# Two attention layers on one core: where the loads for the next batch are issued in layer 1

## The chip, the cores and the metric

The kernel runs on one NeuronCore of a Trainium2 chip. The metric is the time on the device of one execution, in microseconds; lower is better. The kernel before takes 3918.9 us, the median of three runs from 3916.26 to 3920.2 us.

The engines are named as in the profile: PE (TensorE: matrix products), ACT (ScalarE), DVE (VectorE), POOL (GpSimd) and SP (SyncE, which only issues transfers). Sixteen DMA engines move data between DRAM and the on-chip memory (SBUF) and within it.

## The reference

Eight images x of 512 channels and 32 x 32 = 1024 positions go through two residual layers, all in float32. Layer 0 is an ordinary attention with eight heads and does not matter here. Layer 1 is an attention whose heads are mixed before the softmax and normalised after it:

```
q, k, v = einsum('oc,bct->bot', w_q | w_k | w_v, gn(x))      # 8 heads of 64 channels
attn = einsum('bhdq,bhdT->bhqT', q, k) * scale
attn = einsum('gh,bhqT->bgqT', w_head, attn)                 # each head becomes a mix of all eight
attn = softmax(attn, axis=-1)
attn = (attn - mean) / sqrt(var + EPS) * in_gamma + in_beta  # mean and var per image and head
out  = einsum('bhqT,bhdT->bhqd', attn, v).reshape(b, t, c) @ w_proj.T + b_proj
x = x + out
```

## The kernel before, in words

Layer 0 runs from 0 to about 1790 us, layer 1 from there to the end. Layer 1 loops over eight batches b = 0..7 (one image each), and inside a batch over steps p = 0..8 (`step`, called for p and for t = 0..3). A step handles 128 of the 1024 query positions. The steps are numbered from 0 here, as in the code: "step 3" is p = 3, the fourth step of the batch. Work of several query blocks overlaps: in step p the kernel makes the raw scores of block p, mixes and exponentiates block p - 1, and multiplies block p - 2 (and the beginning of p - 1) with the values v.

- `scores(p, i)`, i = 0..7 (L1674): q times k for one pair of heads and one half of the keys. The half is kh = i // 4. ACT copies each result from PSUM into the tile `raw` (L1686), which has one buffer for each half.
- `regroup(p, kh, s)` (L1692): two transfers of 256 KB each, issued by SP, from `raw` to the tile `re`, so that the eight heads of one position come to lie on neighbouring partitions. A step issues 16 of them: three pairs of half 0 at t = 1, one pair at t = 2, four pairs of half 1 at t = 3. Half 1 can be copied only when the last scores of the step are done, so its pairs are issued in fact at the very end of step p and in the first 5 us of step p + 1.
- `mix(p, s)`, s = 0..3 (L1711): PE multiplies `re` with the mixing matrix; ACT takes the exponential (L1724). `mix(p, 0)` is called in step p + 1 at t = 0, behind three scores and a piece of values; it needs the first pair of half 1.
- `flip` (L1739) and `moments` (L1753) on DVE, `values` (L1769) on PE, and `leave` (L1785) on ACT follow.
- At the odd steps 3, 5 and 7, `totals` (L1811 to L1817) makes the reciprocal sums of a pair of blocks, and POOL's queue writes them to DRAM (`zd`, four transfers of 2 KB). `broadcast` (L1829) is written in the program at steps 4, 6 and 8, t = 0 and t = 2, and reads them back as two transfers of 256 KB (`rzb`), also from POOL's queue. POOL does nothing else in between, so it issues them as soon as the four small writes have landed. `divide` (L1856) on POOL uses them.

The order of the work on every engine is the order of the program text, written out by hand in `step`. A small agenda (`ag`) holds extra work with the slot at which it is to run: `y` of the next batch is normalised at step 6, one of its four parts in each t; the k projection of the next batch starts in step 8.

The change is about the loads for the next batch. Each is a closure in the list `pieces`, and `piece(n)` (L1696 to L1700) runs the next n of them. For batches 0 to 6 there are six pieces of 512 KB each: four parts of `y` of the next batch (`y_piece`, L1349) and two of the four parts of its k weights (`left_piece`, L1318, f = 0 and f = 4). The first k piece also takes the tile `left`, whose last reader was the q projection before the batch. The other two parts of the k weights come at step 8 from the agenda. For batch 7 there are four pieces of 256 KB each, the output weights (`p_piece`, L1343). All pieces are issued by SP, at t = 0 of a step, so they stand in SP's queue behind the half-1 regroups of the step before and ahead of the half-0 regroups of their own step.

The setup of the pieces and the loop that calls `step`:

```
a.pieces += [lambda c=c: y_piece(b + 1, c) for c in range(NCC)]
a.pieces += [lambda f=f: left_piece(("k", b + 1), f, 2) for f in (0, 4)]
...
a.pieces += [lambda c=c: p_piece(c) for c in range(NCC)]      # last batch
...
for p in range(NT + 1):
    for t in range(4):
        a.step(p, t, ag)
```

Of the kernel before, what the change touches and what calls it, by code (L numbers as in the profile page):

```python
# [467 lines left out]
def tile_two_attention_layers(  # L468
# [810 lines left out]
    with ExitStack() as l1:  # L1279
# [173 lines left out]
        def k_leave():  # L1453
            for fn in due:
                fn()
            due.clear()
# [203 lines left out]
        class Attention1:  # L1660
# [242 lines left out]
            def step(self, p, t, ag):  # L1903

                new, old, older = p < NT, p >= 1, p >= 2
                if t == 0:
                    if new:
                        for i in range(3):
                            self.scores(p, i)
                            if i == 1:  # L1910
                                ag.run(4 * p - 0.75)
                    if older:
                        self.values(p - 2, 0, 2, 3)
                        self.leave(p - 2, 0)
                        if p % 2:
                            self.sums(p // 2 - 1)
                    ag.run(4 * p - 0.5)
                    k_leave()
                    if old:
                        self.mix(p - 1, 0)  # L1920
                    ag.run(4 * p - 0.25)
                    if p % 2 == 0 and p >= 4:
                        self.broadcast(0)
                elif t == 1:
                    if older:
                        self.values(p - 2, 1, 0)
                        self.flip(p - 1, 0)
                        if p % 2:
                            self.totals(p // 2 - 1)
                        self.moments(p - 1, 0)  # L1930
                    if new:
                        self.scores(p, 3)
                    ag.run(4 * p + 0.5)
                    k_leave()
                    if old:
                        self.mix(p - 1, 1)
                elif t == 2:
                    if p % 2 == 0 and p >= 4:
                        self.broadcast(1)
                    if older:  # L1940
                        self.values(p - 2, 1, 1)
                    if new:
                        self.scores(p, 4)
                        self.scores(p, 5)
                    ag.run(4 * p + 1.5)
                    k_leave()
                    if old and not new:
                        self.mix(p - 1, 2)
                    if older:
                        self.values(p - 2, 1, 2, 3)  # L1950
                        self.leave(p - 2, 1)
                    if old and new:
                        self.mix(p - 1, 2)
                else:
                    if new:
                        self.scores(p, 6)
                        if old:
                            self.values(p - 1, 0, 0)
                        self.scores(p, 7)
                        if old:  # L1960
                            self.mix(p - 1, 3)
                            self.values(p - 1, 0, 1)
                    else:
                        ag.run(4 * p + 2.5)
                        k_leave()
                        self.mix(p - 1, 3)
                        self.values(p - 1, 0, 0, 1)
                if p == 1 or old and t:
                    self.flip(p - 1, t)
                    self.moments(p - 1, t)  # L1970
                if new:
                    first = 3 + (p == 0)
                    for kh, s in (
                        [], [(0, i) for i in range(first)], [(0, i) for i in range(first, 4)],
                        [(1, i) for i in range(4)],
                    )[t]:
                        self.regroup(p, kh, s)
                if t == 3 and p % 2 == 0 and p >= 4:
                    self.divide(p // 2 - 2, nc.gpsimd)
                if older and t == 0:  # L1980
                    self.piece()
                ag.run(4 * p + t)

        def set_flag(pf):
# [172 lines left out]
```

## Time and profile before

| | |
|---|---|
| median of three runs | 3918.9 us (3916.26 to 3920.2) |
| the profiled execution: time, and span of its instructions | 3922.93 us, 3921.2 us |
| PE busy | 3862.0 us, 98% of the span |
| DVE, ACT, POOL busy | 2736.8, 1968.0, 207.3 us |
| transfers issued by SP (queue q1) | 500.08 MB, 45.0% of 16 engines' span |
| transfers issued by POOL (queue q0) | 12.81 MB, 1.6% |
| regroups | 1024 transfers of 256 KB |
| waits of PE in layer 1, from 1820 us on, for a regroup to land | 12.5 us in 14 waits |

How to read it. The span runs from the first to the last instruction of the profiled execution. Busy time says how long an engine had something to do; PE's 98% leaves some 59 us of idle time in the whole kernel. "a <- b" after a group names what ended the wait before it. The share of the DMA engines is the mean over sixteen engines of the time in which they had a packet in hand. Step boundaries are taken at the first score product (L1674) of each step. SP's instructions are all issues and waits, so the landing of its transfers is read from the updates of their semaphores in the trace.

### The profile page before, as it was taken

The numbers are of one execution on the slowest core, as the hardware profiler recorded it, in microseconds if no ns is written. First come the engines' busy times: TensorE is split into PE (matmuls) and PEld (weight loads), VectorE is DVE, ScalarE is ACT, GpSimd is POOL, SyncE is SP. The second block draws the span as 40 slices with busy tenths as digits, with TensorE's granted clock in tenths as the row PEclk, the third lists the DMA queues.
The fourth block names the chain that finished last, engine by engine and source line by source line (L and its number), as shares of the span: only waits on it lengthen the run. The fifth ranks groups of instructions, "written<-read, shape, count | busy, mean of one in ns | idle before, by whom it ended". The sixth has DMA issues, their size and how long they took to land. (4 is left out here: it accounts for less than half of the span.)

```text
span 3921.2 us, 95349 instructions
## 1 busy us (share of the span) xinstructions
PE 3862.0 (98%) x41868; PEld 1818.7 (46%) x41868; DVE 2736.8 (70%) x3729; ACT 1968.0 (50%) x2400; POOL 207.3 (5%) x210
## 2 busy tenths in 40 slices
PE   8999999999999999999999999999999999999999
PEld 4353534344353535344554544535545545445455
DVE  4747576665757474766867858858858768678498
ACT  1726354453627172534725717627438257166175
POOL 0000000000000000000110200201101102002000
PEclk9999999999999999999999999999999999999999
DMA  3313131212121121215947929749659569387396
GB/s 121 120 54 117 49 116 36 71 48 85 55 75 67 49 87 49 90 49 149 235 144 178 243 83 231 200 124 235 187 129 233 158 162 234 107 216 207 120 220 161
DMA packets 249592, 519.07 MB, mean 132 GB/s; under 512 B 51024, under 2 KB 58192, under 8 KB 242512
## 3 DMA queue, kind: packets, MB, share of 16 engines
q1 hardware_dynamic: 241984, 500.08, 45.0%
q0 software_dynamic: 7184, 12.81, 1.6%
q8 instruction: 330, 5.41, 0.6%
q14 instruction: 94, 0.77, 0.1%
HBM read 197.16 MB, written 46.92 MB: 62 GB/s over the span
## 5 line engine op out<-in xcount | busy, mean ns | idle before, releaser
L1739 DVE STREAM_TRANSPOSE et<-e 128x2048 f32<-128x2048 f32 x256 | 590.0, 2305 | 197.4 <-ACT e L1724 196.5
L1769 PEld LDWEIGHTS a<-et,v 128*64 128x64 f32 x16384 | 506.6, 138 | 287.7 <-issue 272.7
L1753 DVE BATCH_NORM_STATS2 bn<-e 128x6 f32<-128x512 f32 x1024 | 635.7, 683 | 0.0
L1093 ACT ACTIVATE e<-s 128x1024 f32<-128x1024 f32 x512 | 497.1, 1026 | 232.7 <-PE s L1088 229.5
L1686 ACT COPY raw<-s 128x1024 f32<-128x1024 f32 x480 | 470.1, 1018 | 234.9 <-PE s L1674 208.7
L1724 ACT ACTIVATE e<-m 128x1024 f32<-128x1024 f32 x512 | 496.3, 1021 | 164.9 <-issue 62.2
L1769 PE MATMUL a<-et,v 128*64 128x64 f32 x16384 | 554.8, 224 | 3.3 <-issue 3.2
L1103 DVE TENSOR_TENSOR zacc<-zacc,e 128x1024 f32<-128x1024 f32 x384 | 468.8, 1221 | 123.7 <-ACT e L1093 99.4
L1674 PE MATMUL s<-k,q 64*64 64x512 f32 x4096 | 514.4, 606 | 2.7 <-DVE v L1046 1.4
L1088 PE MATMUL s<-q,k 64*64 64x512 f32 x4096 | 490.4, 594 | 2.3 <-ACT e L1093 2.3
L1116 PE MATMUL a<-e,v 64*64 64x512 f32 x4096 | 484.1, 589 | 0.0
L1711 PE MATMUL m<-re,wmix 32*32 32x512 f32 x8192 | 304.7, 599 | 17.7 <-DMA re<-raw 12.5
L1116 PEld LDWEIGHTS a<-e,v 64*64 64x64 f32 x4096 | 156.7, 133 | 282.8 <-issue 282.2
L1088 PEld LDWEIGHTS s<-q,k 64*64 64x64 f32 x4096 | 146.4, 133 | 284.3 <-issue 217.8
L1817 POOL DMA_DIRECT2D zd<-rz x96 | 52.5, 552 | 3378.4 <-DMA re<-raw 1862.5
L1674 PEld LDWEIGHTS s<-k,q 64*64 64x64 f32 x4096 | 127.3, 132 | 216.3 <-issue 97.2
L1785 ACT COPY q<-a 64x256 f32<-64x256 f32 x256 | 94.1, 367 | 136.8 <-PE a L1769 135.1
L1711 PEld LDWEIGHTS m<-re,wmix 32*32 32x32 f32 x8192 | 67.9, 103 | 156.6 <-ACT raw L1686 70.6
L1482 PE MATMUL pv_t<-wv,y 128*128 128x512 f32 x256 | 120.6, 608 | 0.0
L906 PE MATMUL pv_p<-left_v,tmp 128*128 128x256 f32 x512 | 114.7, 380 | 2.5 <-DVE tmp L935 2.5
L906 PE MATMUL pk_p<-tmp,left_k 128*128 128x512 f32 x256 | 112.5, 592 | 0.0
L906 PE MATMUL pq_p<-tmp,left_q 128*128 128x512 f32 x256 | 112.5, 592 | 0.0
(325 smaller groups left out, 3838.8 us busy)
## 6 DMA issues: line engine op xcount, KB each, us to landing
re<-raw SPq DMA_DIRECT2D x1024, 256.0 KB
left_q<-left_q SPq DMA_DIRECT2D x17, 1792.0 KB
left_p<-left_p SPq DMA_DIRECT2D x17, 1792.0 KB
left_k<-left_k SPq DMA_DIRECT2D x10, 1792.0 KB
x<-in_x_dram SPq DMA_DIRECT2D x32, 512.0 KB
rzb<-zd SPq DMA_DIRECT2D x128, 128.0 KB
x<-x SPq DMA_DIRECT2D x64, 256.0 KB
y<-x SPq DMA_DIRECT2D x32, 512.0 KB
```

The source lines that it names most:

```text
L906: nc.tensor.matmul(out, st, mv, start=start, stop=(k == 1), skip_group_check=True)
L1088: nc.tensor.matmul(ps[c * D : c * D + D, m], k[r, hp, k0 : k0 + D], q[r, hp, ts(f, FB)], start=True, stop=True,)
L1093: nc.scalar.activation(e[i], ps, AF.Exp, scale=S0 * S0)
L1103: nc.vector.tensor_add(zacc[g], zacc[g], e[i])
L1116: nc.tensor.matmul(acc[g][a][m * D : m * D + D], v[rows, kc, ts(2 * hp + m, D)], e[i][rows, m], start=(kc == 0), stop=(kc == NG - 1),)
L1674: nc.tensor.matmul(ps[c * D : c * D + D, m], qo_t[b][r, p, hp, ts(c, D)], k_t[b][r, hp, ts(kh, FB)], start=True, stop=True,)
L1686: nc.scalar.copy(dst, ps)
L1711: nc.tensor.matmul(ps[a // 2][c * 32 : c * 32 + 32, a % 2].rearrange("p (r h k) -> p h r k", r=2, h=2), wmix[rows].rearrange("p g i -> p ( ...
L1724: nc.scalar.activation(e[:, :, 2 * h : 2 * h + 2].rearrange("p r a k -> p a r k"), ps[h].rearrange("p a (r k) -> p a r k", r=2), AF.Exp,)
L1739: nc.vector.transpose(self.et[p, u].rearrange("p kb (r st a) g q -> p st kb r (a g q)", r=2, st=2)[:, st], self.e[p, s].rearrange("p r a ( ...
L1753: nc.vector.bn_stats(self.bn[n][:, p % 2, s, a], e[:, :, a].rearrange("p r k -> p k r"))
L1769: nc.tensor.matmul(acc[two * D : two * D + D, s].rearrange("p (x q) -> p x q", q=4), v_t[b][:, kb, ts(g, D)], et[:, kb, :, g], start=(kb = ...
```

## The change

One condition in `step`. Before, each step from p = 2 on issued one piece at t = 0, as long as there were any. Now a table says how many pieces each step issues: one at p = 2, two at p = 3, none at p = 4, two at p = 5, none at p = 6, one at p = 7. `piece` itself already took a number.

```diff
                 if t == 3 and p % 2 == 0 and p >= 4:
                     self.divide(p // 2 - 2, nc.gpsimd)
-                if older and t == 0:
-                    self.piece()
+                if t == 0:
+                    self.piece((0, 0, 1, 2, 0, 2, 0, 1, 0)[p])
                 ag.run(4 * p + t)
```

For batches 0 to 6:

| step p | 2 | 3 | 4 | 5 | 6 | 7 |
|---|---|---|---|---|---|---|
| before | y0 | y1 | y2 | y3 | k0 | k4 |
| after | y0 | y1, y2 | - | y3, k0 | - | k4 |

For batch 7: the four parts of the output weights were issued at p = 2, 3, 4, 5, one each; now the first at p = 2, the second and third at p = 3, the fourth at p = 5. Everything else, the number and size of transfers included, is as before.

## The prediction

> **What bounds the kernel now.** I read the page first, then PE's waits in layer 1, then the steps of two batches side by side, then the queues around one stall.
>
> ```profile
> PE 3862.0 (98%) x41868; PEld 1818.7 (46%) x41868; DVE 2736.8 (70%) x3729; ACT 1968.0 (50%) x2400; POOL 207.3 (5%) x210
> ...
> q1 hardware_dynamic: 241984, 500.08, 45.0%
> ```
>
> PE is the bound, so a change of transfers shows only where PE waits. PE's waits from 1820 us on:
>
> ```profile
> PE m L1711 <- DMA re<-raw: 12.5, 14, 2.0
> PE m L1711 <- ACT raw L1686: 4.3, 4, 1.5
> ```
>
> The mix is what waits, and for regroups. Where? The windows of batch 3, one row per step p = 2 to 7:
>
> ```profile
> 2650.60:2671.10 20.50, 20.50 (x451) 11.00 (x450) 19.07 (x22) 16.91 (x21) 0.00 (x0) 1.00 0.91 234
> 2671.10:2692.30 21.20, 21.09 (x457) 11.52 (x454) 19.32 (x24) 16.86 (x21) 3.25 (x6) 1.00 0.98 239
> 2692.30:2714.00 21.70, 20.58 (x452) 11.06 (x448) 18.57 (x21) 16.82 (x21) 2.36 (x1) 1.00 0.93 232
> 2714.00:2734.80 20.80, 20.80 (x458) 11.36 (x454) 19.24 (x24) 16.91 (x21) 3.25 (x6) 1.00 0.97 241
> 2734.80:2758.90 24.10, 22.05 (x456) 11.65 (x452) 20.51 (x22) 17.83 (x22) 2.34 (x1) 0.93 0.88 212
> 2758.90:2780.90 22.00, 21.84 (x490) 12.35 (x490) 20.80 (x26) 18.77 (x23) 2.32 (x5) 1.00 0.90 224
> ```
>
> Columns: window, its length, busy PE, PEld, DVE, ACT, POOL, then the granted clock, the DMA share, GB/s. Batch 4, steps 3 to 6:
>
> ```profile
> 2944.20:2965.00 20.80, 20.80 (x460) 11.36 (x458) 19.24 (x24) 16.91 (x21) 3.26 (x6) 1.00 0.97 245
> 2965.00:2987.30 22.30, 20.81 (x452) 11.18 (x450) 19.04 (x22) 16.78 (x21) 2.36 (x1) 1.00 0.90 225
> 2987.30:3008.10 20.80, 20.80 (x457) 11.35 (x455) 18.85 (x24) 16.93 (x21) 3.25 (x6) 1.00 0.97 242
> 3008.10:3030.40 22.30, 20.78 (x452) 11.44 (x448) 20.00 (x22) 17.81 (x22) 2.35 (x1) 1.00 0.94 227
> ```
>
> The reader is to see a rhythm: in the odd steps 3 and 5 the DMA engines are full (0.97 to 0.98) and PE hardly idles; PE loses 1.1 to 2.05 us in the even step behind each. Why the odd steps are full, in SP's and POOL's timelines:
>
> ```profile
> 2670.66 6.29 SPq L1692 DMA_DIRECT2D re<-raw  x7
> 2677.00 1.04 SPq L1349 DMA_DIRECT2D y<-x  x1
> 2680.62 17.95 SPq L1692 DMA_DIRECT2D re<-raw  x16
> 2698.62 0.63 SPq L1349 DMA_DIRECT2D y<-x  x1
> ```
>
> ```profile
> 2688.73 1.08 POOL L1829 DMA_DIRECT2D rzb<-zd  x2 [4.54 <-DMA re<-raw]
> ```
>
> The broadcasts, written in the even steps, are issued late in the odd ones (2688.73 is in step 3). So 0.5 MB of broadcast joins the 16 regroups and the piece of steps 3, 5 and 7, just ahead of the half-1 regroups. Then PE and ACT at the start of step 4:
>
> ```profile
> 2698.28 1.15 PE L1711 MATMUL m<-re,wmix 32*32 32x512 f32 x32 [1.12 <-DMA re<-raw]
> ```
>
> ```profile
> 2694.49 2.84 ACT L1686 COPY raw<-s 128x1024 f32<-128x1024 f32 x3 [1.04 <-DMA re<-raw]
> ```
>
> Two stalls of one backlog: mix(3,0) waits for the first half-1 pair, and ACT's copies wait until the half-0 regroups have emptied `raw`. By the semaphore updates the first half-1 regroup of steps 2, 3, 4, 5 lands 3.0, 5.9, 3.2, 6.7 us after its issue. And the piece of step 4 is issued at 2698.62, after the stalled mix began at 2698.28: step 4's own piece cannot cause step 4's stall.
>
> **The change part by part.** All edits concern DMAs on SP's queue; none is moved past anything of POOL's.
>
> (a) One piece more in step 3. Transfer time: 45.0% of 3921.2 us is 1764.5 us for 500.08 MB, so a full set of engines moves 283 GB/s and 524,288 B take 1.85 us. Step 3's own row gives less, 239 GB/s at 0.98, hence 2.15 us; I take 1.85, because the pieces' packets are longer than the regroups'. Free room in a full odd step is 0.02 to 0.03 of 21 us, about 0.5 us, mostly after the piece. So everything behind it lands 1.85 - 0.5 = 1.35 us later. Ends: 0.8 (some odd steps show about 1.0 us of room) and 2.15 (no room). The stalled mix and ACT's copies have no slack at the start of step 4 in any batch, so the delay goes to PE one for one.
>
> (b) The same in step 5, onto step 6: 1.35 us. In two of the seven batches step 6 does not stall now, but its pair lands within 0.2 us of the mix, so they pay nearly as much.
>
> (c) Nothing in steps 4 and 6: I cost the relief at nothing. The steps behind them, 5 and 7, have no DMA stall in most batches, and the queue of step 4 runs nearly dry before step 5 (the DMA share falls to about a tenth in its last microsecond in batch 3). So no relief is handed on to the full odd step. The gain could be at most the few tenths by which step 7 waits for a regroup in one batch (0.3 us).
>
> (d) SP's issues. A second issue in steps 3 and 5 takes about 1.0 us. Between the piece (2677.00 plus 1.04) and the next regroup (2680.62) SP waits 2.6 us for ACT; that hides it. Without that cover, half 0 would be issued up to 1 us later. SP waited 0.3 us in all for an earlier regroup of its own queue; a longer backlog can lengthen that, but then the engines already have work queued.
>
> (e) Readers. y is normalised at step 6, so y2 one step earlier helps nobody; k0 is first used in step 8, and its tile is free since the q projection. No new wait.
>
> (f) Batch 7 moves one 256 KB piece from step 4 to step 3: 0.93 us, less 0.5 of room, 0.4.
>
> Sum of transfers: 14 x 1.35 + 0.4 = 19.3 us.
>
> (g) The clock. Batch 3's step 6, with a wait of 2.05 us, shows a granted clock of 0.93 over 24.1 us: 0.07 x 24.1 = 1.7 us lost. The waits of 1.5 us and less stand at 1.00. Waits of mix(p,0) now: step 4 in batches 0 to 6: 1.53, 0.98, 0.96, 1.12, 1.29, 0.93, 1.40; step 6: 0.27, 0.51, 1.00, 2.05, 1.52, 0, 0. With 1.35 on top, all seven of step 4 and three of step 6 exceed 2.05 us; one of those is slowed already. Nine candidates; a single row cannot tell whether each one trips it, and I take six: 6 x 1.7 = 10.2 us. Ends: none, and 13 x 1.7 = 22 (all but the one slowed now).
>
> [...]
>
> [...]
>
> Total: 19.3 + 10.2 = 29.5 us. Against the profiled execution's 3922.93 us that is 3952; that execution lies 4.0 us above the median of the runs, so against the median: 3918.9 + 29.5 = 3948 us, +0.75%.
>
> **The rivals.**
>
> Only one of the two moves costs. Step 5 absorbs its second piece: its first five regroups of half 0 land 4.1 to 5.1 us after issue in batch 3, against 5.5 to 6.3 in step 3, so there is more room. Against it: step 6 stalls today. 7 x 1.35 + 0.4 + 4 x 1.7 = 16.7: 3936.
>
> All of it costs, at the upper ends: 14 x 2.15 + 0.9 + 22 = 53: 3972. For it: step 4 is longer than its mix wait explains (batch 5 loses 3.1 us with a wait of 0.9), as late copies make ACT late too.
>
> No change, under 0.2% or 7.8 us (about what a measurement of this kernel can tell from none): the share counts packets in flight, and the engines have room. For it: short stretches of step 3 move over 350 GB/s. Against it: latency grows in exactly the steps with a broadcast. 3919.
>
> Faster, by one mechanism: the extra piece delays POOL's small zd writes, so the broadcasts are issued behind the half-1 regroups and no longer stand ahead of them. That takes 1.85 us (two times 256 KB) from the odd steps' backlog against 1.35 added: -0.5 x 14 = -7, and -0.9 x 14 = -13 with 1.0 us of room: 3906 to 3912. It decides once the broadcast slips from 2688.73 to past 2691.3, where half 1 starts, by 2.6 us. Against it: they are on another queue, and the whole piece is only 1.85 us.
>
> **How the numbers follow.** Forecast 0.53, one move only 0.20, upper ends 0.12, no change 0.08, faster 0.07. Slower: 0.53 + 0.20 + 0.12 = 0.85. The bounds of (a), (b) and (g) reach from 14 x 0.8 = 11 us, 3930, to 3972. That range holds the forecast, one move and most of the upper ends, about 0.81.
>
> **What would show it.** Right: steps 4 and 6 of batches 0 to 6 grow by 1 to 4 us, steps 3 and 5 keep 20.8 us, PE's waits for regroups rise from 12.5 to about 30 us, the latency of the first half-1 regroup in steps 3 and 5 rises to 7 to 8 us, and the granted clock dips in some even steps. Wrong: (a) if those latencies stay at 6 us; (c) if steps 5 or 7 become shorter; (g) if waits over 2 us stand at a clock of 1.00. I would be wrong in sign if the stalls of step 4 shrank, which would mean that the piece of step 4 took part in them after all.

## The result, and the profile after

The changed kernel takes 3935.06 us (median of 16 runs), the kernel before 3921.14 us (16 runs too). The ratio is 1.0032, with a 95% interval of 1.0024 to 1.0040: about 12.5 us slower (13.9 us by the two medians alone). The prediction was 29.5 us slower. The profiled execution of the changed kernel took 3936.2 us, against 3922.93 us before.

The page of the changed kernel, PE's busy time and the group of the mix:

```profile
PE 3865.1 (98%) x41868; PEld 1819.3 (46%) x41868; DVE 2739.1 (70%) x3729; ACT 1968.0 (50%) x2400; POOL 207.1 (5%) x210
...
L1711 PE MATMUL m<-re,wmix 32*32 32x512 f32 x8192 | 307.1, 603 | 28.6 <-DMA re<-raw 27.8
```

PE's busy time grew by 3.1 us (3862.0 to 3865.1) with the same number of instructions. That is about what the lower clock took: by the clock records of layer 1, PE ran at a clock of 0.5 for two stretches of 3.4 us more than before (three against one), at 1.7 us each. One of the two, at 1821.8 us, stands in step 1 of batch 0, ahead of every moved piece. The other 10 us of the longer span are idle time. Its waits from 1820 us on:

```profile
PE m L1711 <- DMA re<-raw: 27.8, 20, 2.7
PE pk L1391 <- DVE re L1406: 2.8, 7, 0.7
PE a L1769 <- issue: 0.8, 2, 0.4
```

The mixes' wait for regroups went from 12.5 us in 14 waits to 27.8 us in 20, where about 30 us had been forecast. That looks closer than it is: 4.3 us of mix waits that stood under ACT's copies before are now gone from the list. Taken together, whatever ended them, the waits before `mix(3,0)` and `mix(5,0)` rose from 15.0 to 25.9 us, by 10.9 us. Steps 2 to 7 of batch 3 (window, length, busy PE, PEld, DVE, ACT, POOL, granted clock, DMA share, GB/s):

```profile
2658.60:2679.10 20.50, 20.50 (x451) 11.00 (x449) 19.07 (x22) 16.91 (x21) 0.00 (x0) 1.00 0.95 234
2679.10:2700.10 21.00, 21.00 (x460) 11.46 (x456) 19.45 (x24) 16.91 (x21) 3.25 (x6) 1.00 1.02 258
2700.10:2722.80 22.70, 20.55 (x451) 11.05 (x448) 18.44 (x21) 16.79 (x21) 2.34 (x1) 1.00 0.88 206
2722.80:2743.70 20.90, 20.90 (x460) 11.42 (x457) 19.30 (x24) 16.95 (x21) 3.25 (x6) 1.00 1.04 262
2743.70:2765.60 21.90, 20.52 (x450) 11.05 (x448) 19.47 (x22) 17.74 (x22) 2.34 (x1) 1.00 0.84 211
2765.60:2787.60 22.00, 21.84 (x490) 12.30 (x488) 20.82 (x26) 18.77 (x23) 2.19 (x4) 1.00 0.91 224
```

and steps 3 to 6 of batch 4:

```profile
2951.00:2971.90 20.90, 20.90 (x460) 11.45 (x458) 19.24 (x24) 16.90 (x21) 3.26 (x6) 1.00 1.05 261
2971.90:2996.30 24.40, 21.93 (x454) 11.58 (x452) 18.67 (x21) 16.83 (x21) 2.34 (x1) 0.93 0.83 191
2996.30:3018.00 21.70, 21.26 (x456) 11.53 (x454) 19.83 (x25) 17.50 (x22) 3.25 (x6) 1.00 1.04 260
3018.00:3040.20 22.20, 20.85 (x456) 11.17 (x452) 19.77 (x21) 17.21 (x21) 2.34 (x1) 1.00 0.86 200
```

The rhythm is the one of before, with both strokes stronger. The odd steps still last about 21 us, but their rate is now 258 to 262 GB/s instead of 239 to 245, and their DMA share reads 1.02 to 1.05. So 0.98 before was not a ceiling: the share adds up the times of all packets in flight, and in step 3 of batch 3 the packet records show up to 22 at once on the sixteen engines (20 before). Step 3 of batch 3 moved 258 x 21.0 = 5.42 MB instead of 239 x 21.2 = 5.07 MB; two thirds of the added 0.52 MB went through within the step. The even steps wait for the rest.

SP's, POOL's and PE's timelines around the same stall:

```profile
2678.66 6.17 SPq L1692 DMA_DIRECT2D re<-raw  x7
2684.88 1.92 SPq L1349 DMA_DIRECT2D y<-x  x2
2688.63 17.79 SPq L1692 DMA_DIRECT2D re<-raw  x16
```

```profile
2698.31 1.06 POOL L1829 DMA_DIRECT2D rzb<-zd  x2 [6.12 <-DMA zd<-rz]
```

```profile
2707.07 1.15 PE L1711 MATMUL m<-re,wmix 32*32 32x512 f32 x32 [2.15 <-DMA re<-raw]
```

The two pieces go out together, in SP's pause before the half-0 regroups, as expected. The wait of this mix grew from 1.12 to 2.15 us. And the broadcast now waits 6.12 us for the zd writes and starts 19.2 us after the step's start, instead of 17.6. Over the batches its mean start moved from 16.8 to 18.4 us in step 3 and from 16.6 to 18.6 us in step 5.

One measure is used in all that follows: how late `mix(3,0)` and `mix(5,0)` start in steps 4 and 6, as a mean over the eight batches. It is the start of the mix after the first score product of its step, less 4.75 us, the value where it does not wait. Before: 1.24 us in step 4 and 0.76 us in step 6. After: 1.58 and 1.80. Each is one profiled execution, and such means scatter: kernels with one piece in the odd step and broadcasts at 16.6 to 18.7 us give 0.61 to 1.24 us, here and in what follows. The lengths of the steps scatter too. Between these two profiles step 6 grew from 21.6 to 22.6 us on average, while step 4, which was to grow by 1 to 4 us, took 22.3 us in both. In the experiments with the halves and with held broadcasts it takes 22.9 to 23.2 us behind two pieces and 21.3 to 22.1 us behind one.

### The profile page after: what moved, and what is told of

Read it like the earlier page. It is cut to its first block, busy times and chain, and to the rows that moved or that the text cites. A ratio compares the mean times of both kernels' runs of the same rounds, so it can differ in the third digit from the quotient of the medians.

```text
span 3934.4 us, 95349 instructions
## 1 busy us (share of the span) xinstructions
PE 3865.1 (98%) x41868; PEld 1819.3 (46%) x41868; DVE 2739.1 (70%) x3729; ACT 1968.0 (50%) x2400; POOL 207.1 (5%) x210
## 5 line engine op out<-in xcount | busy, mean ns | idle before, releaser
L1711 PE MATMUL m<-re,wmix 32*32 32x512 f32 x8192 | 307.1, 603 | 28.6 <-DMA re<-raw 27.8
```

The source lines that it names most:

```text
L1711: nc.tensor.matmul(ps[a // 2][c * 32 : c * 32 + 32, a % 2].rearrange("p (r h k) -> p h r k", r=2, h=2), wmix[rows].rearrange("p g i -> p ( ...
```

## The experiments

My theory after the result: a piece costs through the half-1 regroups behind it (backlog), only with more room than I had given it. The rival: it costs or saves through the slip of the broadcasts.

### The halves, the opposite, and a larger dose

Only the table was edited; the diffs are against the changed kernel.

```diff
-                    self.piece((0, 0, 1, 2, 0, 2, 0, 1, 0)[p])
+                    self.piece((0, 0, 1, 2, 0, 1, 1, 1, 0)[p])   # y2 alone moved
+                    self.piece((0, 0, 1, 1, 1, 2, 0, 1, 0)[p])   # k0 alone moved
+                    self.piece((0, 0, 2, 0, 2, 0, 2, 0, 0)[p])   # all in even steps
+                    self.piece((0, 0, 0, 3, 0, 3, 0, 0, 0)[p])   # three and three
```

> Only the first half of the change: y2 moves from step 4 to step 3, k0 stays in step 6 (pieces per step 1, 2, 0, 1, 1, 1 for steps 2 to 7). Backlog theory (each extra 512 KB in an odd step delays the first half-1 regroup of that step by about 1.35 us, and the next even step pays it): half of the 12.6 us, so +6 us, 3926, all of it in step 4. Slip theory (the extra piece also delays the small zd writes, so the broadcasts slip behind and give back most of the cost; in the one profile of the changed kernel the mixes of step 4 are only 0.3 us later each, 2.7 us in all): +2 to +3 us, 3923. In both, step 6 stays as before, with mix waits of about 6 us over the eight batches.

Measured: 1.0011 (1.0002 to 1.0020), 3931.36 against 3927.06 us. Step 4's mix is 1.90 us late, step 6's 0.82 us.

> Only the second half of the change: k0 moves from step 6 to step 5, y2 stays in step 4 (pieces per step 1, 1, 1, 2, 0, 1). Backlog theory: +6 us, 3927, in step 6. Slip theory, from the one profile (the mixes of step 6 are 8.4 us later in all): +8 to +10 us, 3930, in step 6; step 4 as before. If the two halves together do not make up +12.6 us, they act on each other.

Measured: 1.0018 (1.0008 to 1.0029), 3934.09 against 3927.06 us. Step 4's mix is 0.89 us late, step 6's 1.67 us. Each half acts only on the step behind it, and 0.11% and 0.18% add up to 0.29%, against 0.32% for both. My reading from one profile that the y2 half costs next to nothing did not hold: alone it makes step 4's mix as late as the k0 half makes step 6's.

> The opposite of the change: two pieces each in steps 2, 4 and 6, none in steps 3, 5 and 7 (batch 7: two in steps 2 and 4). Backlog theory: the even steps have 1.5 to 2.5 us of free room on the DMA engines, enough for a second piece of 1.85 us, and the odd ones lose 1.85 us of work, so the mix waits of steps 4 and 6 (16 us in all) mostly vanish: -8 to -14 us, 3907 to 3913. Slip theory: without a piece in the odd steps the broadcasts are issued earlier, ahead of the half-0 tail, and take back part: -2 to -6 us, 3916. Rival (any step with two pieces stalls, whichever it is): +10 us, 3931.

Measured: 1.0016 (1.0004 to 1.0028), 3932.18 against 3927.06 us: slower, not faster. Both theories missed this; the rival had the sign, at twice the size. PE's waits in this kernel:

```profile
PE m L1711 <- DMA re<-raw: 10.9, 17, 2.1
PE a L1769 <- issue: 4.0, 9, 1.0
```

With no piece in steps 3 and 5, the mixes behind them are still 0.91 and 0.83 us late, within the scatter of the kernels with one piece there. So taking the first piece out of an odd step freed nothing that can be told. A second piece stood in the even steps instead, so this run does not part the two. Of the even steps, 2 and 6 lost 3.6 and 3.4 us over the eight batches; step 4 did not.

> A larger dose: three pieces in step 3 and three in step 5, none elsewhere (batch 7: three and one). Backlog theory: one piece more than in the changed kernel in each of the two steps, at 1.85 us each with the free room used up: +26 us over the changed kernel, 3961, and several clock dips of 1.7 us, as nearly every wait would be over 2.5 us. Slip theory: the broadcasts slip once more by 1.5 to 2 us, to behind the first half-1 regroups, and the third piece costs little: +5 us over the changed kernel, 3940.

Measured: 1.0089 (1.0075 to 1.0104), 3960.18 against 3927.06 us. That is 33 us over the kernel before, and about 20 us over the changed one: nearer to the backlog theory's 26 than to the slip theory's 5. Steps 3 to 6 of batch 3:

```profile
2690.00:2712.10 22.10, 21.82 (x460) 11.47 (x456) 19.81 (x25) 16.91 (x21) 3.24 (x6) 1.00 1.04 271
2712.10:2736.30 24.20, 21.96 (x451) 11.61 (x448) 18.30 (x20) 16.80 (x21) 2.34 (x1) 0.93 0.81 191
2736.30:2758.20 21.90, 21.24 (x462) 11.63 (x459) 20.09 (x25) 17.69 (x22) 3.24 (x6) 1.00 1.04 269
2758.20:2780.60 22.40, 20.52 (x448) 11.22 (x447) 18.52 (x21) 17.01 (x21) 2.43 (x1) 1.00 0.85 211
```

At 269 to 271 GB/s the odd steps no longer take the third piece without loss: they grow themselves, by 0.7 us each on average, and step 4 shows a clock of 0.93. The doses side by side, lateness of the mix behind an odd step with so many pieces:

| pieces in the odd step | 0 | 1 | 2 | 3 |
|---|---|---|---|---|
| step 3, seen in step 4 | 0.91 | 1.24, 0.89 | 1.58, 1.90 | 2.32 |
| step 5, seen in step 6 | 0.83 | 0.76, 0.82 | 1.80, 1.67 | 2.27 |

Two numbers in a cell are two kernels, each from one profile. The second piece costs 0.67 us in step 3 (means 1.07 to 1.74) and 0.95 us in step 5 (0.79 to 1.74).

### Without the broadcasts

```diff
+                if self.zn < NCH - 1:
+                    if t == 0:
+                        nc.gpsimd.memset(self.rzb, 1.0)
+                    return
                 self.zq.dma_start(
```

> The kernel before with the broadcasts of the first three pairs of blocks left out: rzb is filled with 1.0 by one POOL instruction instead, so those blocks are not divided by their sums. Broadcast theory: it is the 0.5 MB of broadcast that fills steps 3, 5 and 7; without it the first half-1 regroup of steps 3 and 5 lands about 4.5 us after its issue, as in steps 2 and 4, instead of 6.4 to 6.9, and the mix waits of steps 4 and 6 (16 us in all) go: -14 to -20 us. Rival (the regroups of the odd steps are late for another reason, so a kernel without pieces in the odd steps kept waits of 0.9 us): less than 5 us gained and latencies above 6 us.

Measured: 0.9958 (0.9944 to 0.9973), 3907.98 against 3923.21 us.

```profile
PE m L1711 <- DMA re<-raw: 0.9, 3, 0.3
```

> The changed kernel with the same broadcasts left out. Broadcast theory: the second piece of steps 3 and 5 then finds about 2 us of room and costs 0 to 3 us against the kernel before without broadcasts. Rival (two pieces in one step stall by themselves): it still costs +10 to +13 us against that kernel.

Measured: 0.9958 (0.9941 to 0.9974), 3905.79 us.

```profile
PE m L1711 <- DMA re<-raw: 1.4, 4, 0.4
```

This settles the partner of the collision. Without the broadcasts the waits for regroups all but vanish in both kernels, the first half-1 pair of steps 3 and 5 lands 4.6 to 4.7 us after its issue instead of 6.4 to 7.6, and the change is worth nothing (-2.2 us by the medians, the same ratio). In this kernel a second piece in the odd steps cost 12.5 us with the broadcast in the same steps, and nothing without it.

### When the broadcasts are issued

In the kernel before, POOL fills rzb six or thirteen times before the first two broadcasts of a batch:

```diff
+                    for _ in range(6 if self.zn < NCH - 2 else 0):
+                        nc.gpsimd.memset(self.rzb, 1.0)
                 self.zq.dma_start(
```

> The kernel before, with its pieces as they were; only the broadcasts of steps 3 and 5 come later: POOL first fills rzb six times with 1.0 (0.97 us each), so that it issues them about 18.9 us after the step's start instead of 16.7, about as late as the two-piece kernel does by itself (18.4 to 18.6). Slip theory (the later issue is what gives back part of a second piece's cost): the mixes of steps 4 and 6 come 0.4 to 1 us earlier each, -6 to -14 us, 3909 to 3917 on a chip where the kernel before takes 3923. Rival (the issue time of the broadcasts does not matter while it is ahead of the half-1 regroups at 19.8; the second piece is cheap because there was free room): 0 +- 3 us.

Measured: 1.0036 (1.0022 to 1.0049), 3939.88 against 3925.08 us. The broadcasts start at 19.5 to 19.7 us; the mixes are 1.46 and 1.02 us late. A later broadcast did not help here. At this place it meets the first half-1 regroups, issued from 19.8 us on; that this is the reason was not tried. The mean granted clock of these runs, 0.9978 against 0.9990, accounts for 4.6 of the 14.8 us.

> The same with thirteen fills: the broadcasts of steps 3 and 5 are issued about 25.7 us after the step's start, which is 5 us into the next step and behind all half-1 regroups. Slip theory: the even steps lose their waits as they do without broadcasts: -12 to -18 us, 3905 to 3911. Rival (the broadcasts cost the same wherever they stand): 0 +- 3 us. A later POOL could delay nothing else, since divide is needed only at the end of the batch.

Measured: 1.0026 (1.0015 to 1.0037), 3936.68 against 3925.08 us. The half that was expected happened: with the broadcasts 5 us into the even steps the mixes are 0.05 and 0.00 us late. But the time went up. PE's waits:

```profile
PE a L1769 <- issue: 6.0, 7, 1.8
PE m L1711 <- issue: 4.9, 8, 1.1
PE s L1674 <- issue: 3.3, 2, 2.5
```

These are waits for nothing that the profile names: 14.2 us, where the kernel before has 3.7 us of them:

```profile
PE a L1769 <- issue: 3.2, 4, 1.6
PE m L1711 <- issue: 0.5, 2, 0.2
```

One of the waits behind thirteen fills, in PE's timeline:

```profile
3261.24 1.09 PE L1674 MATMUL s<-k,q 64*64 64x512 f32 x7
3264.84 0.59 PE L1674 MATMUL s<-k,q 64*64 64x512 f32 x1 [2.51 <-issue]
```

It stands in the middle of a run of eight score products that need nothing new. In the packet records, a 16 KB packet of the instruction queue starts 2.7 us before PE goes on. Of the 71 such waits over 0.3 us in layer 1 (from 1820 us on) of the sixteen profiles with broadcasts, 64 end 2.4 to 3.3 us after the start of such a packet. These packets came only every 6.4 us (median), and a moment taken at random fell into such a stretch in 11% of cases. That PE was waiting for its own code, which came late, is my guess from these records; no run shows it by itself. The thirteen fills are not needed for such waits: with a piece and the broadcasts together in the even steps and no fills at all (the two kernels with one piece further below) they come to 8.1 and 8.5 us.

### The broadcasts held at one time

To part the piece from the slip, the broadcasts were made independent of the zd writes:

```diff
+                src = self.zd[t].rearrange("g i -> (g i)")
+                if self.zn < NCH - 2:
+                    src = x1_d[self.b][t]
                 self.zq.dma_start(
                     out=self.rzb[t * D : t * D + D],
-                    in_=self.zd[t].rearrange("g i -> (g i)").partition_broadcast(D),
+                    in_=src.partition_broadcast(D),
                 )
```

with four fills (first two runs) or five (last two) ahead of them, as above.

> The kernel before, with the broadcasts of steps 3 and 5 made independent of the small zd writes: they read two rows of layer 1's input instead of the reciprocal sums, so those blocks are scaled wrongly, and POOL fills rzb four times with 1.0 (3.9 us) to issue them at about 17.0 us of the step whatever SP's queue holds. It is the control for the next run: 0 to +5 us against the kernel before, mix waits of 0.8 to 1.3 us in steps 4 and 6.

Measured: 0.9994 (0.9985 to 1.0003), 3923.0 against 3927.23 us.

```profile
PE m L1711 <- DMA re<-raw: 11.6, 15, 1.7
```

> The changed kernel with the same fixed broadcasts. Theory of the shifted broadcast (the second piece costs because it delays the zd writes and with them the broadcasts, from 16.7 to 18.5 us, and the first half-1 pair lands about 5 us after the middle of the broadcast): with the broadcast held at 17.0 us the cost is gone, 0 to +4 us against the control. Backlog theory (the piece's own 1.85 us of transfer, partly hidden, is what delays the half-1 regroups): +10 to +14 us against the control, as without the holding.

Measured: 1.0043 (1.0029 to 1.0056), 3940.87 us, 17.9 us over the control.

```profile
PE m L1711 <- DMA re<-raw: 26.4, 17, 2.6
```

The broadcasts start at 17.4 us in both. The cost stays with the broadcast held, so the theory that the piece acts by shifting the broadcast falls, and the piece's own transfer is what is left. The mixes go from 0.61 and 0.98 us late to 1.81 and 1.88, that is 1.20 and 0.90 us per step.

> As the control with fixed broadcasts, but with five fills instead of four, so that the broadcasts are issued at about 18.4 us of steps 3 and 5 instead of 17.4, where the changed kernel has them by itself. If a later broadcast helps: 0 to -5 us against the control at 17.4. If it hurts by itself, as the run with six fills suggested (19.5 us, +14.8 us): +5 to +10 us.

Measured: 0.9999 (0.9991 to 1.0008), 3925.61 against 3925.93 us, with broadcasts at 18.4 us.

> The changed kernel with the broadcasts held at about 18.4 us. If the slip from 16.7 to 18.5 us is what made the change cost 12.6 us rather than the 17.9 us measured with broadcasts at 17.4 us: 3933 to 3936 (on a chip where the kernel before takes about 3923 to 3927), 4 to 6 us faster than the changed kernel at 17.4 us. If the slip gives nothing back and the two differ by the source of the broadcast or by the chip: 3940 or more, as at 17.4 us.

Measured: 1.0041 (1.0028 to 1.0054), 3942.15 us, 16.5 us over its own control. So between 17.4 and 18.4 us the start of the broadcasts makes no difference that can be told, neither to one piece nor to two; the slip gave nothing back. The mixes go from 1.13 and 1.16 us late to 1.84 and 1.88, by 0.71 and 0.72 us. It is not shown that the change costs more with held broadcasts (17 us) than without (12.5 us). The intervals overlap: 1.0024 to 1.0040 for the change, and for these two pairs some 1.0033 to 1.0065 and 1.0027 to 1.0057, when the two intervals of a pair are added in squares. Much of what lies between them is clock. By the granted clocks of all runs, the changed kernel loses 6.3 and 6.6 us more than its control in these pairs, and about 2.8 us more in the kernel as it is. The profile of the last run shows six dips of the clock in steps 3 to 6, its control none.

### The broadcasts in the even steps

SP issues the broadcasts, in the order of the program:

```diff
-                self.zq.dma_start(
+                nc.sync.dma_start(
                     out=self.rzb[t * D : t * D + D],
```

> The kernel before with the broadcasts issued by SP instead of POOL (the small zd writes stay on POOL). SP keeps the program's order, so the first goes out in step 4, 6 or 8 behind the half-1 regroups of the step before, and the second behind three pairs of half-0 regroups. Broadcast theory: the odd steps hold 16 regroups and one piece only, the even ones also the broadcasts: 0.5 MB moves out of the full steps, -10 to -16 us, 3907 to 3913; the even steps then are the full ones and their successors may wait 0 to 1 us. Rival (any full step stalls the next): 0 to +5 us.

Measured, with one piece in each step: 1.0025 (1.0014 to 1.0036), 3934.39 against 3925.08 us. Steps 4 and 6 now hold 16 regroups, a piece and the broadcasts, and the steps behind them, 5 and 7, wait: their mixes are 0.90 and 0.99 us late.

> The changed kernel with the broadcasts issued by SP. Now the odd steps hold two pieces and the even steps the two broadcasts and no piece. Broadcast theory: this is the even spread, so it is as fast as without broadcasts, 3904 to 3908, -15 to -19 us against the kernel before, and 0 to 8 us faster than one piece in each step with SP's broadcasts. The same change that cost 12.6 us would then gain. Rival (two pieces in a step always cost): 5 to 13 us slower than one piece in each step with SP's broadcasts.

Measured, with the changed table: 0.9971 (0.9959 to 0.9982), 3914.77 us: 10.3 us faster than the kernel before, and 19.6 us faster than one piece in each step. SP's timeline in steps 3 and 4 of batch 3:

```profile
2670.62 6.16 SPq L1692 DMA_DIRECT2D re<-raw  x7
2676.82 1.88 SPq L1349 DMA_DIRECT2D y<-x  x2
2680.58 18.36 SPq L1692 DMA_DIRECT2D re<-raw  x16
2699.05 1.03 SPq L1829 DMA_DIRECT2D rzb<-zd  x1
2702.68 4.88 SPq L1692 DMA_DIRECT2D re<-raw  x6
2707.66 1.54 SPq L1829 DMA_DIRECT2D rzb<-zd  x1
```

Two pieces in the odd step, two broadcasts in the even one. The windows of steps 3 to 6 of that batch:

```profile
2671.10:2693.20 22.10, 22.01 (x457) 11.54 (x455) 19.30 (x24) 16.86 (x21) 2.12 (x4) 1.00 0.96 240
2693.20:2714.10 20.90, 20.60 (x455) 11.08 (x452) 18.59 (x21) 16.96 (x21) 0.00 (x0) 1.00 0.97 227
2714.10:2735.20 21.10, 21.10 (x456) 11.52 (x454) 19.29 (x24) 16.93 (x21) 4.50 (x5) 1.00 1.00 253
2735.20:2756.10 20.90, 20.61 (x451) 11.07 (x449) 19.35 (x22) 17.87 (x22) 0.00 (x0) 1.00 0.96 229
```

The even steps are down to 20.9 us; the shares are even, 0.96 to 1.00.

In this kernel step 7 and what follows grew by 0.5 to 1.4 us a batch, so a last pair gave the third broadcast of a batch back to POOL:

```diff
-                nc.sync.dma_start(
+                (nc.sync if self.zn < NCH - 2 else self.zq).dma_start(
```

> The changed kernel with the first two broadcasts of a batch issued by SP (behind the half-1 regroups) and the third by POOL as before, since step 7 and what follows grew by about 1.1 us a batch when SP issued that one too. Broadcast theory: steps 3 to 6 without DMA waits and steps 7 and 8 as before: 8 us faster than with all three on SP, about 3907, -18 us against the kernel before. Rival (the 1.1 us come from elsewhere): 3915.

Measured: 0.9975 (0.9966 to 0.9984), 3914.5 against 3923.08 us. The third broadcast was not the reason: step 7 and the rest still take about 1 us more a batch (128.5 to 129.1 us, before 127.6 to 127.9). The traces show where PE loses it: before L1807, the products in `totals`, it waits 1.1 us a batch for DVE's `moments` and ACT's exponentials, against 0.1 us before. Why these come later stays open.

> The kernel before with the same two broadcasts on SP: one piece in every step from 2 to 7. It tells what the change is worth where the broadcasts stand in the even steps. Theory of the fullest step (the even steps now hold 16 regroups, a piece and the broadcasts, and steps 5 and 7 pay): +2 to +6 us against the kernel before, 15 to 20 us slower than the changed kernel with the same broadcasts. Rival (the broadcasts alone decide, the pieces do not matter): the same time as the changed kernel with these broadcasts.

Measured: 1.0044 (1.0031 to 1.0058), 3937.15 us: 22.6 us slower than the changed table with the same broadcasts. Of this, 7.1 us lie in PE's waits without a named cause, 8.5 us here against 1.4 us (8.1 against 1.0 us in the pair with all broadcasts on SP). The pieces do matter, and their best place depends on where the broadcasts stand: the same edit loses 12.5 us in the kernel as it is, and gains 20 to 23 us with the broadcasts one step later.

## Why the prediction was right or wrong

The direction, the place and the mechanism were right; the size was 2.4 times too large. Two terms of the sum were mis-sized, each by some 7.5 to 8.5 us: the delay by a second piece in (a) and (b), and the clock dips in (g). Step by step, with the letters of the prediction:

- What bounds: right. The broadcasts fill the odd steps and the even ones pay; without broadcasts the mixes' waits for regroups came to 0.9 and 1.4 us instead of 12.5 and 27.8, and the change cost nothing (-2.2 us).
- (a) and (b), 1.35 us for each of 14 steps, 18.9 us: mis-sized. The step that failed is the free room of an odd step, "0.02 to 0.03 of 21 us, about 0.5 us", read off the DMA share as if 1.00 were full. The same steps then ran at 1.02 to 1.05 and 258 to 262 GB/s, and at 271 GB/s with three pieces. The lateness measured is 0.67 us behind step 3 and 0.95 us behind step 5, 14 x 0.81 = 11.3 us. So about 1.0 us of the piece's 1.85 us was absorbed. With the broadcasts held the lateness was 1.20 and 0.90 us in one pair of kernels, 0.71 and 0.72 us in the other. The sign named for this in the prediction came out between right and wrong: the first half-1 regroup of steps 3 and 5 landed 6.4 and 6.6 us after its issue (median), against 6.0 and 5.2 us before, and not 7 to 8.
- (b), that steps without a stall pay nearly as much: right; step 6 of batches 5 and 6, without a wait before, waited 2.4 and 1.6 us.
- (c), no relief from the emptied even steps: right. Steps 5 and 7 did not become shorter, and the halves alone showed cost in the step behind and no gain elsewhere beyond the scatter.
- (d) and (e): right; both issues, 1.92 us, fit into SP's pause ahead of the half-0 regroups (3.75 us), and no new wait on SP or a reader appeared.
- (g), six clock dips, 10.2 us: the other step that failed, in number. Dips behind long waits there are, but steps 3 to 6 of the changed kernel's profile show two, where the kernel before has one: 1.7 us more. The granted clocks of all runs say about 2.8 us: 7.1 us lost in the mean of the 16 changed runs, 4.3 us in that of the 104 runs of the kernel before beside the experiments (each clock is given to three places). Two things were wrong. The waits stayed shorter than 1.35 us would have made them, with five over 2.05 us instead of ten. And not every such wait was followed by a dip: in the eighteen profiles, PE's waits in layer 1 (from 1820 us on) were followed within 7 us by a dip to half the clock, for 3.4 or 6.8 us, in none of 134 cases of 0.7 to 1.7 us, in 6 of 22 up to 2.05 us, in 7 of 20 up to 2.4 us, and in 16 of 21 above that. Three of the five waits over 2.05 us here stood at a clock of 1.00, such as the 2.15 us shown above; the prediction had named this as the sign that (g) is wrong.

With the measured terms the sum is 11.3 us and 1.7 to 2.8 us for the clock, 13.0 to 14.1 us, against 12.5 us by the ratio and 13.9 us by the medians. The terms come from single profiles that scatter, so an agreement this close is partly luck.

- The rivals. "Only one of the two moves costs" gave 3936 and so came nearest in time, for the wrong reason: both halves cost, each about half of what I had given. "Upper ends" and "no change" are out. "Faster" had its first half: the broadcasts did slip, by 1.6 to 2.0 us, short of the 2.6 us named. (Its upper figure, -13 us at 1.0 us of room, should read -14 by its own numbers: with that room the piece adds 0.85 us, and 1.85 less 0.85 is 1.0 us for each of 14 steps.) But even behind the half-1 regroups, where the lateness of the mixes vanished, the kernel was slower, as PE then waited elsewhere.

## What to carry to other kernels

Place a transfer by what the queue really issues in that step, not by where the program text has it: the broadcasts, written in the even steps, ran in the odd ones (16.8 and 16.6 us after the start of steps 3 and 5), because POOL had nothing to hold it back, and the table that avoids the even steps was therefore the wrong one for this kernel and the right one once SP's queue held the broadcasts in place. A DMA share near 1.00 was no ceiling here: the odd steps, at 0.97 to 0.98 and 239 to 245 GB/s before, ran at 1.02 to 1.05 and 258 to 262 GB/s with one piece more. So bound the room by the rate that the same engines reach elsewhere in the kernel's own traces, and count from them too how many waits of PE are followed by a dip of the clock: here 23 of the 41 waits over 2.05 us were, at 1.7 us for each 3.4 us of half clock. And test a placement by removing its partner in the collision before moving more load about: here it showed at once that 15 us of the kernel hung on three broadcasts of 0.5 MB a batch.

## What the hardware showed that I had not expected

- A broadcast of 0.5 MB went along with a loss of PE's time in places that need none of its data: with the broadcasts 5 us into the even steps, the waits without a named cause rose from 3.7 to 14.2 us, and 64 of 71 such waits in the profiles with broadcasts ended 2.4 to 3.3 us after the start of a 16 KB instruction packet.
- Taking out the first piece of an odd step gained nothing that can be told, the second cost 0.7 to 0.95 us, the third about 0.5 us of lateness and 0.7 us of the odd step itself; the transfer alone would be 1.85 us, by the prediction's estimate from 283 GB/s.
- Emptying the full steps of their pieces did not help: with no piece in steps 3 and 5, and two in the even steps, the mixes behind them were 0.91 and 0.83 us late, about as with one.
